# Latent attention: scores over high and low halves of q and k

## The chip, the cores and the metric

The kernel runs on one core of a Trainium2 chip. The metric is device time in microseconds (us) of one execution. A core has TensorE (PE in the profile, its weight loads PEld), VectorE (DVE), ScalarE (ACT), GpSimd (POOL) and SyncE (SP), which issues most DMAs. Each engine runs its own queue in order, and engines wait for each other by semaphores.

## The reference

The input is x, 8 sequences of 1024 tokens with 256 channels. A latent attention with 16 heads of width 16 is followed by a two-layer stack of windowed attention and gated MLP. The kernel normalises a token before each of the two parts and adds the part's result to its input. Cut to the part that the change touches:

```python
c_kv = x @ W_kv_down                                   # 256 -> 128
k_rope = rotary(c_kv @ W_k_rope)                       # 32 wide, shared by the heads
k = (c_kv @ W_k_up).reshape(B, T, 16, 16)
v = (c_kv @ W_v_up).reshape(B, T, 16, 16)
q = (x @ W_q).reshape(B, T, 16, 16)
q_rope = rotary(x @ W_q_rope)
scores = einsum('bqhd,bkhd->bhqk', q, k) + einsum('bqr,bkr->bqk', q_rope, k_rope)[:, None]
w = softmax(where(causal, -inf, scores / sqrt(48)))
out = einsum('bhqk,bkhd->bqhd', w, v).reshape(B, T, 256) @ W_o
```

## The kernel before

Two stages follow each other: `mla` (L155 on) does the latent attention of all 8 sequences, `local` the two layers after it. The end of `mla` and the start of `local` overlap. After both, a test over values collected on the way decides whether a general version is run as well; with these inputs it is not.

The exponential of a sum of scores is taken as a product: `rotary` (L402) computes the rotary scores, which all heads share, and ACT writes their exponentials into `er` once per block of 128 keys; a second exponential with the opposite sign (L409) serves the test alone, and both are summed along the way into `most` and `least`. POOL zeroes the masked triangle. For each head, `scores` (L421) makes the 16-wide products on PE, ACT takes the exponential into `pt` (L437), `turned` (L441) multiplies `pt` by `er` on DVE (L451), and `values` (L453) multiplies by v on PE (L462). v has a column of ones, so the sum of weights falls out beside the result; `finished` and `turn_back` divide by it and transpose on DVE, `out_add` multiplies by W_o and adds to x.

A unit of work is one or two of (c, g, kb): c is the half of the queries (512 columns), g a group of four heads, kb a block of 128 keys. Scores are transposed: keys on the partitions, queries along the columns. Four heads' products go at once to PE, each in its own 32 rows. As a head has 16 rows, keys are kept twice, in tiles `k` whose other 16 rows are zero (the mask of L372), so that one 32-row strip of q serves two heads. Blocks at the causal edge have 384, 256 or 128 query columns and are packed in pairs into one unit.

There are 36 units a batch (a batch is one sequence), 24 single and 12 paired, and one step of the loop takes one unit: the scores of unit s, then the multiplication of unit s-1, then the values of unit s-2, then what the table `beside` lists for this step. The table holds all other work of this sequence and of the next (who = 0 or 1; 2 loads and statistics of the one after it; -1 the output of the one before): normalisation, transposes, projections, rotary scores, output. PE, DVE, ACT and POOL keep the written order (`manual_schedule`); SP's order is left to the scheduler.

PSUM sets the ties between steps: a step's scores fill two tiles of two banks (`pscore`), which the exponentials of the step before must have left; everything listed in `beside` shares two single banks (`psum1`, by `bank`) in turn. `pt` has six buffers. All projections are cut by `times` (L198) into four matmuls of 32 columns of weights, which also run at once. During the second half of the last sequence, when no next one is prepared, the two single banks become a third score tile.

Of the kernel before, what the change touches and what calls it, by code (L numbers as in the profile page):

```python
# [29 lines left out]
F32 = mybir.dt.float32  # L30
AF = mybir.ActivationFunctionType
ALU = mybir.AluOpType
# [3 lines left out]
P = 128  # L36
# [45 lines left out]
def preln_mla_local_kernel(  # L82
# [72 lines left out]
    def mla(ctx: ExitStack, verdict):  # L155
# [85 lines left out]
        wq = wp.tile([P, 2, 2, 4, 2, HD], F32, name="wq")  # L241
        wk = wp.tile([P, 2, 4, 2, HD], F32, name="wk")
        mask = wp.tile([P, 2], F32, name="mask")
        for e in range(2):
            nc.vector.tensor_reduce(
                mask[:, e : e + 1], ident.rearrange("p (r e d) -> p r e d", e=2, d=HD)[:, :, e, :], AX.XY, ALU.add
            )
        for m in range(2):
            for e in range(2):
                cols = slice(128 * m + 64 * e, 128 * m + 64 * e + 64)  # L250
                nc.scalar.copy(
                    wq[:, :, m, :, e, :], wqnat[:, :, cols].rearrange("p c (r d) -> p c r d", d=HD)
                )
                nc.scalar.copy(wk[:, m, :, e, :], wknat[:, cols].rearrange("p (r d) -> p r d", d=HD))
        wq = wq.rearrange("p c m r e d -> p c m (r e d)")
        wk = wk.rearrange("p m r e d -> p m (r e d)")


# [10 lines left out]
        most = wp.tile([P, B * 12], F32, name="most")  # L269
        least = wp.tile([P, B * 12], F32, name="least")  # L270

        class Batch:


            def __init__(self, b):
                self.b = b
                self.sums = {}
# [4 lines left out]
            def statistics(self, n, part):  # L282
# [17 lines left out]
                self.found.append((mv, rstd))  # L300

            def normalise(self, n, part):
                mv, rstd = self.found[n]
                if part == 0:
                    if n == 0:
                        self.xn = []
                    self.xn.append(p1.tile([P, 4, D], F32, tag="xn", name=f"xn{self.b}_{n}", bufs=3))
                xn = self.xn[n]
                for i in (2 * part, 2 * part + 1):
                    nc.vector.tensor_scalar(  # L310
                        xn[:, i, :], self.x[:, 4 * n + i, :], mv[:, i, 0:1], rstd[:, i : i + 1],
                        ALU.subtract, ALU.mult,
                    )
# [40 lines left out]

            def query(self, m, n, c, part=None):
                if m == 0 and n == 1 and c == 0 and not part:
                    self.q = of[self.b % 2].tile([P, 2, T], F32, tag="q", name=f"q{self.b}")
                ps = self.dense(f"psq{m}_", [wq[:, 0, m, :], wq[:, 1, m, :]], self.xnc, n, c, part)
                if ps is not None:
                    on_a(self.q[:, m, HALF[n]], ps)  # L360

            def keys(self, m, n, part=None):

                if n == 0 and not part:
                    if m == 0:
                        self.k = []
                    for e in range(2):
                        g = 2 * m + e
                        self.k.append(of[self.b % 2].tile([P, T], F32, tag=f"k{g}", name=f"k{self.b}_{g}"))
                ps = self.dense(f"psk{m}_", [wk[:, m, :]], [self.ckvT], n, 0, part)  # L370
                for e in range(2) if ps is not None else ():
                    nc.scalar.activation(  # L372
                        self.k[2 * m + e][:, HALF[n]], ps, AF.Identity, scale=mask[:, e : e + 1]
                    )

# [26 lines left out]
            def rotary(self, c, kb):  # L402
# [3 lines left out]
                n = 12 * self.b + 8 * (1 - c) + kb  # L406
                nc.scalar.activation(er, ps[:, :w], AF.Exp, scale=SCALE, accum_out=most[:, n : n + 1])  # L407

                nc.scalar.activation(ps[:, :w], ps[:, :w], AF.Exp, scale=-SCALE, accum_out=least[:, n : n + 1])  # L409
                if q0 == kb * P:  # L410
# [3 lines left out]
                    )  # L414

# [5 lines left out]
            def scores(self, key, parts):  # L421
# [3 lines left out]
                for c, g, kb in parts:  # L425
                    q0, w, _ = self.block(c, kb)
                    for n in range(4):
                        rows = slice(32 * n, 32 * n + 32)
                        nc.tensor.matmul(  # L429
                            two[n // 2][:, n % 2, lo : lo + w], self.k[g][rows, kb * P : (kb + 1) * P],  # L430
                            self.q[rows, g // 2, q0 : q0 + w], start=True, stop=True,
                        )
                    lo += w
# [40 lines left out]
            def finished(self, c, g, oT):  # L474


                nat = late.tile([P, 16, 32], F32, tag="onat", name=f"onat{self.b}_{c}_{g}", bufs=3)
# [40 lines left out]
        for step, who, *what in (  # L518
            (0, -1, "out_add", 6, 1, 1), (0, 0, "query", 1, 1, 0),
            (1, 0, "query", 1, 1, 1),  # L520
            (2, 0, "value", 2),
            (3, 0, "keys", 1, 0), (3, 0, "keys", 1, 1, 0), (3, 1, "statistics", 1, 1),
            (4, 0, "keys", 1, 1, 1), (4, 0, "query", 0, 0, 0), (4, 1, "normalise", 0, 0),
            (5, 0, "query", 0, 0, 1), (5, 1, "normalise", 0, 1),
            (6, -1, "out_add", 0, 0), (6, 1, "normalise", 1, 0),
# [1314 lines left out]
```

## Time and profile before

| | us |
|---|---|
| median of 3 runs | 3347.74 (3345.59 to 3348.41) |
| span of the profiled execution | 3347.4 |
| scores of the first step, first record | 31.18 |
| one sequence in the steady part of `mla` (403.84 to 525.17) | 121.33 |
| PE, DVE, ACT, POOL busy in that stretch | 120.33, 107.69, 96.93, 9.49 |
| PE busy with L429, the scores, in that stretch | 45.34 |
| PE, DVE, ACT, POOL busy in the whole span | 3270.7, 2686.0, 1713.1, 1341.6 |

A sequence of `mla` thus takes 121 us and its 36 steps some 3.4 us each. The ends of matmuls are modelled in the profile and overlap the next start, so the time from one group's start to the next one's says more than a busy time. A matmul of fp32 operands shows as two records. A line of groups gives the line of code, the engine, the tiles written and read, the shapes and the count, then the busy time and the mean of one in ns, then the idle time ahead and what ended it. In shapes such as 32*128 the first number is the rows of the array in use, the second its columns.

### The profile page before, as it was taken

To read this page: it belongs to the slowest core of one execution; us is meant where nothing else is said; L and a number is where in the kernel's file an instruction comes from. 1 tells how busy PE (TensorE), PEld (TensorE's weight loads), DVE (VectorE), ACT (ScalarE), POOL (GpSimd) and SP (SyncE) were. 2 spreads that over 40 slices of the span, in tenths; PEclk is the share of its full clock that TensorE was granted. 3 is DMA by queue.
4 is the path that set the end of the run, shared out by engine and by line. 5 is a ranking of instruction groups with operands and counts; after the bars stand their busy time and mean duration, and the time that the engine had idled before them with its cause. 6 is when DMAs were issued, how large, how long until landed. Compare 5 with 4: busy or idle time off the path is not lost.

```text
span 3347.4 us, 79461 instructions
## 1 busy us (share of the span) xinstructions
PE 3270.7 (98%) x33826; PEld 1777.5 (53%) x33826; DVE 2686.0 (80%) x3993; ACT 1713.1 (51%) x2238; POOL 1341.6 (40%) x1031
## 2 busy tenths in 40 slices
PE   8999999999987899999999999999999999999998
PEld 2433333333333556666565666566666566665665
DVE  5888888888897887888878887777878778787773
ACT  6878878877862244434444434444444444344441
POOL 1000000000006655655655555555555555555540
PEclk9999999999998899999999999999999999999999
DMA  1000000000032444445344354444545444454431
GB/s 63 8 20 27 8 20 27 8 20 14 14 105 81 115 114 120 123 115 143 105 121 127 113 136 130 137 127 136 134 134 139 121 126 130 124 148 119 109 107 58
DMA packets 369290, 311.74 MB, mean 93 GB/s; under 512 B 154607, under 2 KB 333214, under 8 KB 368798
## 3 DMA queue, kind: packets, MB, share of 16 engines
q1 hardware_dynamic: 366942, 304.16, 33.1%
q8 instruction: 268, 4.39, 0.6%
q10 hardware_dynamic: 1984, 2.41, 0.2%
q14 instruction: 96, 0.79, 0.1%
HBM read 165.96 MB, written 140.51 MB: 92 GB/s over the span
## 4 chain that ended last, share of the span: by engine, by line
PE 90%; DVE 3%; ACT 2%; DMA 1%; issue 1%; SPq 1%; POOL 1%; ACTq 0%; DVEq 0%
PE ag L1088 17%; PE pair L859 13%; PE sc L429 9%; PE psy L1129 8%; PE acc L462 8%; PE psw L1005 7%; PE o L972 6%; PE pv L886 6%; PE pair L931 4%; PE psq L200 2%; PE psx L200 2%; PE s L980 2%; PE psR L200 2%; DVE pt L451 1%; PE psy L1135 1%
## 5 line engine op out<-in xcount | busy, mean ns | idle before, releaser
L451 DVE TENSOR_TENSOR pt<-pt,er 128x1024 f32<-128x1024 f32 x576 | 674.8, 1217 | 77.8 <-ACT pt L437 77.8
L437 ACT ACTIVATE pt<-sc 128x1024 f32<-128x1024 f32 x576 | 560.7, 1029 | 174.0 <-PE sc L429 161.6
L1088 PE MATMUL ag<-d,l 128*128 128x512 f32 x1408 | 640.4, 597 | 1.2 <-DVE xs L1009 0.8
L873 POOL TENSOR_TENSOR t<-t,t 128x1024 f32<-128x1024 f32 x128 | 302.0, 2360 | 792.0 <-DVE t L869 792.0
L937 ACT ACT_TABLE_LOAD x120 | 154.0, 1283 | 702.0 <-PE pair L931 702.0
L859 PE MATMUL pair<-l_qkv,xT 128*128 128x512 f32 x1024 | 469.2, 601 | 5.5 <-DMA xT<-zx 2.4
L1088 PEld LDWEIGHTS ag<-d,l 128*128 128x128 f32 x1408 | 262.2, 190 | 310.2 <-issue 278.1
L125 POOL TENSOR_TENSOR rn<-ss,half 128x16 f32<-128x16 f32 x128 | 373.4, 2917 | 13.7
L429 PE MATMUL sc<-q,k 32*128 32x512 f32 (+3 forms) x3072 | 369.9, 522 | 5.1 <-ACT pt L437 5.0
L462 PE MATMUL acc<-pt,v 128*32 128x512 f32 (+3 forms) x3072 | 332.9, 496 | 4.8 <-DVE pt L451 4.6
L859 PEld LDWEIGHTS pair<-l_qkv,xT 128*128 128x128 f32 x1024 | 193.7, 192 | 248.8 <-issue 207.6
L864 ACT ACTIVATE sq<-pair 128x1024 f32<-128x1024 f32 x128 | 131.0, 1023 | 333.2 <-issue 269.1
L866 DVE TENSOR_TENSOR t<-pair,l_cos 128x1024 f32<-128x1024 f32 x128 | 156.2, 1220 | 157.4 <-ACT sq L864 156.7
L1129 PE MATMUL psy<-l,hid 128*128 128x256 f32 x1280 | 281.5, 379 | 0.0
L1101 DVE SCALAR_TENSOR_TENSOR hid<-ag,l_b,ge 128x512 f32<-128x512 f32 x160 | 115.9, 724 | 196.3 <-ACT ge L1100 171.3
L1129 PEld LDWEIGHTS psy<-l,hid 128*128 128x128 f32 x1280 | 243.2, 190 | 46.7 <-issue 15.1
L937 ACT ACTIVATE pt<-pair 128x1024 f32<-128x1024 f32 (+1 forms) x256 | 234.9, 968 | 56.7 <-PE pair L931 55.4
L429 PEld LDWEIGHTS sc<-q,k 32*128 32x128 f32 x3072 | 157.3, 184 | 199.9 <-ACT pt L437 154.3
L411 POOL TENSOR_SCALAR_AFFINE_SELECT er<-er 128x128 f32<-128x128 f32 x64 | 51.5, 804 | 524.0 <-ACT er L407 524.0
L879 POOL TENSOR_TENSOR t<-t,rn 128x1024 f32<-128x1024 f32 x128 | 249.2, 1947 | 10.0
L972 PEld LDWEIGHTS o<-pt,v 128*32 128x32 f32 x7680 | 201.6, 110 | 88.0 <-issue 82.0
L886 PE MATMUL pv<-l_qkv,xT 128*128 128x512 f32 x512 | 240.6, 592 | 0.0
(132 smaller groups left out, 4876.8 us busy)
## 6 DMA issues: line engine op xcount, KB each, us to landing
z<-turned SPq DMA_DIRECT2D x512, 128.0 KB, 2.4
qkT<-z SPq DMA_DIRECT2D x128, 512.0 KB, 3.7
y<-xs SPq DMA_DIRECT2D x128, 128.0 KB, 2.6
h<-y SPq DMA_DIRECT2D x32, 512.0 KB, 4.0
zx<-turneds SPq DMA_DIRECT2D x120, 128.0 KB, 2.7
xT<-zx SPq DMA_DIRECT2D x240, 64.0 KB, 2.6
zh<-turnedh SPq DMA_DIRECT2D x120, 128.0 KB, 2.3
d<-zh SPq DMA_DIRECT2D x30, 512.0 KB, 3.2
```

The lines of the kernel that those rows point to most:

```text
L125: nc.gpsimd.tensor_tensor(out_, in_, half[:, :n], ALU.pow)
L429: nc.tensor.matmul(two[n // 2][:, n % 2, lo : lo + w], self.k[g][rows, kb * P : (kb + 1) * P], self.q[rows, g // 2, q0 : q0 + w], start=Tr ...
L437: nc.scalar.activation(pt, sc, AF.Exp, scale=SCALE)
L451: nc.vector.tensor_tensor(t, t, er.to_broadcast([P, 1024 // w, w]), ALU.mult)
L462: nc.tensor.matmul(self.acc[g][32 * n : 32 * n + 32, q0 - c * 512 :], self.v[:, kb, h * VW : h * VW + 32], pts[n // 2][:, n % 2, lo : lo + w],
L859: nc.tensor.matmul(qk[:, n].rearrange("p h d -> p (h d)"), self.left(i)[c], w["qkv"][:, c, n * INNER : (n + 1) * INNER], start=(c == 0), s ...
L873: nc.gpsimd.tensor_tensor(t1, t1, t2, ALU.add)
L886: nc.tensor.matmul(pv, self.left(i)[c], self.w["qkv"][:, c, 2 * INNER :], start=(c == 0), stop=(c == 1))
L937: nc.scalar.activation(pt[:, :, : n * P], flat[:, :, : n * P], AF.Exp, scale=-1.0)
L972: nc.tensor.matmul(o[32 * j : 32 * j + 32, g, a, :], vs[m][:, h * DH + a * 32 : h * DH + a * 32 + 32], pts[m][g][:, place(j), off : off + ...
L1088: nc.tensor.matmul(ps.rearrange("p (s a t) -> p s a t", a=4, t=32), w["1"][:, c, i, :], d[:, c], start=(c == 0), stop=(c == 1),)
L1129: nc.tensor.matmul(ps[:, t, :], hid[:, i, cols], w["2"][:, i, :], start=(t == i == 0), stop=False)
```

## The change

- q and k are split in two. The projection's result is copied to a float32r tile (`halves`), which holds the high half; one step later (`low`) TensorE adds minus that half to the same PSUM bank, a matmul with the negative unit matrix `minus`, and what is left is copied as the low half.
- Both halves are then moved by DMA from SP's queue (`place_q`, `place_k`) into tiles of another layout: a head's 32 rows hold high and low parts of k row by row in turn, and for q the same part twice. `scores` makes two float32r products per head, over the low part of q and then the high one, in place of one fp32 product. The masked copies of k and the rearranged weights `wq` and `wk` are gone.
- The normalisation moves from DVE to ACT, with a shift that POOL computes.
- The second exponential of `rotary` and both accumulated sums are gone; in their place squares of the rotary parts (`squares`, ACT) are summed by PE and reduced by DVE (`reach`) once a sequence.
- `xn` and `onat` have two buffers in place of three, and the table lists the projections anew, with `low` entries that are done right after the step's scores.

```diff
+        minus = wp.tile([P, P], F32R, name="minus")
+        nc.scalar.mul(minus, ident, -1.0)
...
+                shift = small.tile([P, 4], F32, tag="shift", name=f"shift{b}_{n}")
+                nc.gpsimd.tensor_tensor(shift, mv[:, :, 0], rstd, ALU.mult)
+                nc.gpsimd.tensor_scalar(shift, shift, -1.0, None, ALU.mult)
+                self.found.append((shift, rstd))
...
                 for i in (2 * part, 2 * part + 1):
-                    nc.vector.tensor_scalar(
-                        xn[:, i, :], self.x[:, 4 * n + i, :], mv[:, i, 0:1], rstd[:, i : i + 1],
-                        ALU.subtract, ALU.mult,
+                    nc.scalar.activation(
+                        xn[:, i, :], self.x[:, 4 * n + i, :], AF.Identity, scale=rstd[:, i : i + 1],
+                        bias=shift[:, i : i + 1],
                     )
...
+            def halves(self, ps, then, *args):
+                t = p1.tile([P, 2, 512], F32R, tag="halves", name=f"halves{self.b}_{then.__name__}{args}", bufs=2)
+                on_a(t[:, 0], ps)
+                self.pending = ps, t, then, args
+
+            def low(self):
+                ps, t, then, args = self.pending
+                nc.tensor.matmul(ps, minus, t[:, 0], start=False, stop=True, skip_group_check=True)
+                on_a(t[:, 1], ps)
+                then(t.bitcast(F32), *args)
...
+            def place_q(self, t, m, n):
+                for g in (2 * m, 2 * m + 1):
+                    q = of[g % 2].tile([P, 2, 512], F32, tag=f"q{g}{n}", name=f"q{self.b}_{g}_{n}")
+                    for s in range(2):
+                        nc.sync.dma_start(q[s : P : 2], t[64 * (g % 2) : 64 * (g % 2) + 64])
+                    self.q[g, n] = q.bitcast(F32R)
...
-                for e in range(2) if ps is not None else ():
-                    nc.scalar.activation(
-                        self.k[2 * m + e][:, HALF[n]], ps, AF.Identity, scale=mask[:, e : e + 1]
-                    )
+                self.halves(ps, self.place_k, m, n)
+
+            def place_k(self, t, m, n):
+                for g in (2 * m, 2 * m + 1):
+                    k = of[self.b % 2 if (m, n) == (0, 0) else 0].tile(
+                        [P, 512], F32, tag=f"k{g}{n}", name=f"k{self.b}_{g}_{n}"
+                    )
+                    for s in range(2):
+                        nc.sync.dma_start(k[s : P : 2], t[64 * (g % 2) : 64 * (g % 2) + 64, s])
+                    self.k[g, n] = k.bitcast(F32R)
...
-                nc.scalar.activation(er, ps[:, :w], AF.Exp, scale=SCALE, accum_out=most[:, n : n + 1])
-
-                nc.scalar.activation(ps[:, :w], ps[:, :w], AF.Exp, scale=-SCALE, accum_out=least[:, n : n + 1])
+                nc.scalar.activation(er, ps[:, :w], AF.Exp, scale=SCALE)
...
+            def squares(self, n):
+                t = (self.rq, self.rk)[n]
+                sq = p1.tile([P, T], F32, tag="xn", name=f"sq{self.b}_{n}", bufs=2)
+                nc.scalar.activation(sq, t, AF.Square)
+                self.sq = getattr(self, "sq", []) + [sq]
+
+            def reach(self):
+                ps = bank(f"reach{self.b}")
+                for i, four in enumerate(QUARTER):
+                    nc.tensor.matmul(ps[four], ones, self.sq[i // 2][:, HALF[i % 2]], start=True, stop=True)
+                nc.vector.tensor_reduce(norms[:, self.b : self.b + 1], ps, AX.X, ALU.max)
...
-                    for n in range(4):
-                        rows = slice(32 * n, 32 * n + 32)
-                        nc.tensor.matmul(
-                            two[n // 2][:, n % 2, lo : lo + w], self.k[g][rows, kb * P : (kb + 1) * P],
-                            self.q[rows, g // 2, q0 : q0 + w], start=True, stop=True,
-                        )
+                    k = self.k[g, kb // 4][:, kb % 4 * P : (kb % 4 + 1) * P]
+                    q = self.q[g, c][:, :, q0 - c * 512 :]
+                    for h in (1, 0):
+                        for n in range(4):
+                            rows = slice(32 * n, 32 * n + 32)
+                            nc.tensor.matmul(
+                                two[n // 2][:, n % 2, lo : lo + w], k[rows], q[rows, h],
+                                start=(h == 1), stop=(h == 0),
+                            )
...
-            (3, 0, "keys", 1, 0), (3, 0, "keys", 1, 1, 0), (3, 1, "statistics", 1, 1),
-            (4, 0, "keys", 1, 1, 1), (4, 0, "query", 0, 0, 0), (4, 1, "normalise", 0, 0),
-            (5, 0, "query", 0, 0, 1), (5, 1, "normalise", 0, 1),
-            (6, -1, "out_add", 0, 0), (6, 1, "normalise", 1, 0),
...
+            (2, 0, "low"), (2, 0, "value", 2),
+            (3, 0, "keys", 1, 0), (3, 1, "statistics", 1, 1),
+            (4, 0, "low"), (4, 0, "keys", 1, 1), (4, 1, "normalise", 0, 0),
+            (5, 0, "low"), (5, 0, "query", 0, 0, 0), (5, 1, "normalise", 0, 1),
+            (6, 0, "query", 0, 0, 1), (6, 1, "normalise", 1, 0),
+            (7, 0, "low"), (7, -1, "out_add", 0, 0), (7, -1, "out_add", 0, 1),
...
+            (10, 0, "query", 1, 0, 0), (10, 1, "normalise", 1, 1),
+            (11, 0, "query", 1, 0, 1), (11, 1, "turn", 0, 0),
+            (12, 0, "low"), (12, 0, "rotary", 0, 0), (12, 1, "turn", 0, 1),
...
+            (22, 1, "query", 0, 1, 0, 1), (22, 1, "query", 0, 1, 1), (22, 1, "squares", 0),
+            (23, 1, "low"), (23, 1, "keys", 0, 0), (23, 2, "statistics", 0, 0), (23, 1, "squares", 1),
+            (24, 1, "low"), (24, 1, "value", 0),
...
+            (27, 1, "low"), (27, 1, "rotary", 1, 0),
...
-            (32, 0, "out_add", 4, 1),
+            (32, 0, "out_add", 4, 1), (32, 1, "reach"),
```

## The prediction

> **What bounds the kernel now.** I read the page's totals first, then the stages, the groups, the timeline of one step and the waits.
>
> ```profile
> PE 3270.7 (98%) x33826; PEld 1777.5 (53%) x33826; DVE 2686.0 (80%) x3993; ACT 1713.1 (51%) x2238; POOL 1341.6 (40%) x1031
> PE 90%; DVE 3%; ACT 2%; DMA 1%; issue 1%; SPq 1%; POOL 1%; ACTq 0%; DVEq 0%
> ```
>
> The chain that ended last is TensorE's, and the lines concerned (L429, L462, L200) work only in the first 1000 us. The busy times of stretches there (columns: stretch, length, then busy time of each engine; 121.33 us from 403.84 is one whole batch, the next two lines split a batch into steps 4 to 25 and steps 26 to 3, the last is the tail of the last batch):
>
> ```profile
> 100.00:900.00 800.00, 793.99 (x8576) 312.34 (x8572) 707.64 (x891) 640.11 (x993) 59.86 (x65) 1.00 0.05 17
> 403.84:525.17 121.33, 120.33 (x1298) 47.25 (x1297) 107.69 (x138) 96.93 (x150) 9.49 (x10) 1.00 0.06 19
> 416.99:491.56 74.57, 73.57 (x781) 27.69 (x777) 64.93 (x80) 56.07 (x79) 4.76 (x5) 1.00 0.07 23
> 491.56:538.32 46.76, 46.76 (x524) 19.56 (x520) 42.76 (x59) 40.86 (x73) 4.73 (x5) 1.00 0.04 13
> 940.00:1000.00 60.00, 51.16 (x406) 17.36 (x404) 54.35 (x79) 37.13 (x43) 3.94 (x6) 0.94 0.48 146
> ```
>
> PE is full in every stretch, but DVE stands at 89% and ACT at 80% right behind, DVE at 91% in steps 26 to 3. In the tail DVE is at 91% and PE is not full: nothing taken from PE helps there. A plain step in the timeline (start, length, engine, line):
>
> ```profile
> 479.06 1.14 PE L429 MATMUL sc<-q,k 32*128 32x512 f32 x8
> 480.13 1.07 PE L462 MATMUL acc<-pt,v 128*32 128x512 f32 x8
> 480.23 1.94 ACT L437 ACTIVATE pt<-sc 128x1024 f32<-128x1024 f32 x2 [1.41 <-PE sc L429]
> 481.01 1.47 PE L200 MATMUL psq<-xnT,wq 128*32 128x256 f32 x16
> 482.42 0.74 PEld L429 LDWEIGHTS sc<-q,k 32*128 32x128 f32 x16 [0.84 <-ACT pt L437]
> ```
>
> Taken from start to start, four heads' scores (4 fp32 products, 8 records) take 1.07 us, their values 0.88, projections 1.41; the exps take 1.94 and start 1.17 after the scores. Per step DVE multiplies twice (L451, 1217 ns each, 2.31 for a pair back to back). One batch by groups (busy, mean ns):
>
> ```profile
> L451 DVE TENSOR_TENSOR pt<-pt,er 128x1024 f32<-128x1024 f32 x73 | 85.5, 1216 | 7.6 <-ACT pt L437 7.6
> L437 ACT ACTIVATE pt<-sc 128x1024 f32<-128x1024 f32 x72 | 70.0, 1029 | 20.6 <-PE sc L429 20.4
> L429 PE MATMUL sc<-q,k 32*128 32x512 f32 x192 | 29.6, 640 | 0.0
> ```
>
> **What the Trainium skill says.** "TensorE: Matmul & The Clock Gate", section "Back-to-back issue gap": a warm matmul of N columns takes N/2.4 + 2.5 ns, 216 for 512. The trace's fp32 product is two records (192 for the batch's 24 groups of four heads at 512 columns), and a quad of value records (four column groups at once) takes 0.88/2 = 0.44 us, about twice that: fp32 costs some 427 per record. Same page, "LDWEIGHTS (loading the stationary operand)": columns/1.2 ns, 107 for 128. The score quad takes 0.535 = 0.427 + 0.108, so it agrees, and these loads aren't hidden. The rate of float32r is shown by no run here: it is the large unknown. "ScalarE: Activation LUTs", section "What ACT_TABLE_LOAD costs": 186 + 0.833 per column ns, 93 more for each per-partition operand, 93 of overlap. The trace agrees: copies of 512 at 593, the masked key copy (one such operand) at 693.
>
> **The change, part by part (per batch; 36 steps).**
>
> 1. *Scores.* 48 groups of four heads: 24 of 512 columns, 8 each of 384, 256 and 128. Each goes from two fp32 quads to two float32r quads; the weight loads stay. If float32r streams a column per cycle, a 512 quad falls from 0.535 to 0.216 + 0.107 = 0.32 and the saving per quad is N/2.4: 24×2×0.213 + 8×2×(0.160+0.107+0.053) = 10.2 + 5.1 = 15.4 us. Ends: 0 (as fast as an fp32 record), and a loss of 41 (as slow as a whole fp32 product: each quad doubles; sum now about 24×1.07 + 8×(0.85+0.64+0.43) = 41). I take the column per cycle: a full fp32 product is made here of two double-priced records[...]. Narrow groups (128) could be slower; 1 us or so.
> 2. *The low halves.* 8 matmuls 128x128x512 float32r: 0.216 + 0.107 + 0.1 assumed for the change of tile shape (0 to 0.2) = 0.42, so +3.4. Each waits for ACT's copy of the step before and stands ahead of values on PE; that copy comes before the step's exps in ACT's queue, so I cost the wait at 0, about 0.6 (one copy) if it is late.
> 3. *reach*: 4 fp32 matmuls, one 512 quad pair, +0.9 on PE, +0.7 on DVE (as L346, 0.69). Splitting projections anew moves PE work between steps, sum unchanged.
> 4. *DVE*: normalise leaves (8×406 ns, 2.9 busy in this batch): 107.7 − 2.9 + 0.7 = 105.5.
> 5. *ACT*: the second exp of rotary and all accumulator reads leave (64 groups' sum: 29.9+8.1+6.8+4.8+21.2 and 22.0 over 8 batches, −11.6); the masked key copies and q copies leave (40.7+19.0 over 8, −7.5); 16 half copies come at 593 (+9.5), eight normalisations at 186+213+186−93 = 0.49 (+3.9), two squares of 1024 at 1.03 (+2.1). Sum 96.9 − 3.6 = 93.3.
> 6. *POOL*: two small operations per four tiles, a step or more ahead of use; 0. *DMA*: 32 moves a batch on SP's queue, 16 of 256 KB and 16 of 128 KB, 6 MB in 115 us where the DMA share is 0.06. Moves of 256 KB land in 2.4 us here (x2d<-x); four at once I put at 6. First use comes 8 steps or more (25 us) after the low half. SP's stores and loads of x now stand among them: each waits on work already due. The halves buffers (two) are rewritten about two steps after their DMAs started (6 us): tight only for the second keys, at most 1 us. So 0 to 1.
>
> PE's sum: 121.3 − 15.4 + 3.4 + 0.9 = 110.2; DVE 105.5; ACT 93.3. PE still leads, but three queues in order, tied within a step, don't reach the largest sum. Taking the two halves of a batch:
>
> - Steps 26 to 3 (14 steps): these hold three of a batch's four pairs of closing transposes, three of four statistics and two of four output additions. PE falls to 46.8 − 14×0.43 + 2×0.42 + 0.9 = 42.5, DVE is 42.8 + 0.7 = 43.5 and becomes the bound; the values of a step come two steps after its scores, which lets PE lead DVE by some 2 us. 41.5 to 44: gain 2.8 to 5.3.
> - Steps 4 to 25 (22 steps): PE is 74.6 − 16×0.43 − 6×0.43 + 6×0.42 = 67.7. Two costs come on top. At step 12 the rotary scores take the bank that this step's low copy frees, and with two banks in turn PE waits for ACT behind both exps: about 3.2 us after the step's start instead of 1.9, 1.2. And ACT is overfull in steps 4 to 6 (exps 1.94, two half copies 1.14, two normalisations 0.98: 4.06, 3.5, 3.5, against PE's 2.9, 2.9, 2.5) and 22 to 24 (two squares, 10.7 against 8.7): 4.8 in all, of which perhaps 1 is absorbed each time, so 0 to 3. Total 69 to 72: gain 2.6 to 5.6.
>
> Per batch 5.4 to 10.9, taken 8.2. Seven batches and the first 16 steps of the last one count, 7.4: 61 us. The start: the rotary part before the first step is held up by ACT (idle of 0.4 to 0.8 on PE after psR), whose work halves there; against that stand two squares, the half copies and the DMA before the first scores. I take 0, ±4. The tail and the local layers stay. The profiled span is 3347.4, the median 3347.7: 3347.7 − 61 = 3287.
>
> **The rivals.**
>
> A. *float32r streams no faster than an fp32 record* (or slower): step 1 gives nothing, PE is 121.3 + 8×0.63 + 0.9 + 1.2 = 128.5, 7.2×7.4 = +53: 3400; at the whole product's price another 41×7.4, near 3700. It ends slower from the point where a 512 quad costs over some 0.48 (the additions are 5.5, spread over 96 quads of 370 columns on average). For: nothing here prices it. Against: the argument of one pass. 0.14. (That the new test of norms fails and sends the run into the general path, is under 0.01 in it: the inputs' largest sum of squares over the rotary rows is about 147, the limit 271.)
>
> B. *The engines' ties eat the gain*: ACT's full steps and DVE's closing steps add up unabsorbed, the halves' buffers wait for DMAs. The waits show that PE and ACT already wait for each other in most steps:
>
> ```profile
> ACT pt L437 <- PE sc L429: 135.5, 158, 2.2
> PEld sc L429 <- ACT pt L437: 120.6, 200, 0.8
> ```
>
> 2 to 5 a batch: 3312 to 3335, about 3325. 0.13.
>
> C. *The ties loosen*: shorter scores let the exps start 0.5 earlier (a loop of 1.94 + 0.55 in place of 1.17), so ACT's fullness is absorbed and PE leads DVE freely. The bound is then the larger sum, about 108: 13×7.4 = 98, 3250. 0.13.
>
> **How the numbers follow.** Forecast 0.60, its own range 3262 to 3312. Range 3245 to 3342: the forecast, all of B (0.13) and half of C (0.065) make 0.80; left out are A and C's lower half. A change of under 0.2% (7 us) can't be told from none in this kernel. Faster: 0.60 + 0.13 of C + 0.12 of B; same 0.01, B's rest; slower A's 0.14.
>
> **What would show it.** Scores L429's successor: start to start 0.65 for a 512 group; if about 1.07, A. Low matmuls about 0.4 each. A batch period of 110 to 116. DVE over 95% busy in steps 26 to 3; PE's idle before rotary at step 12, and before scores in steps 5 to 7 and 23 to 25, released by ACT. No wait of scores on q's or k's DMA past the first step; if there is one, the DMA term was wrong. The local layers equal within 1 us.

## The result and the profile after

The changed kernel takes 3294.14 us (median of 4 runs, 3292.07 to 3297.83), the kernel before 3346.91 beside it: a ratio of 0.984, 95% interval 0.983 to 0.986. The profiled execution has a span of 3290.3 against 3347.4, so 57.1 us are to be found between the two traces.

The totals of the page and the shares of the chain that ended last, after:

```profile
PE 3196.2 (97%) x33762; PEld 1763.2 (54%) x33762; DVE 2668.6 (81%) x3934; ACT 1712.4 (52%) x2055; POOL 1342.9 (41%) x1064
PE 84%; DVE 6%; ACT 4%; DMA 2%; issue 2%; SPq 1%; POOL 0%; ACTq 0%; DVEq 0%
```

TensorE gives up 6 points of the chain to DVE, ACT, DMA and issue. By stretches (columns as in the prediction: stretch, length, busy time of PE, PEld, DVE, ACT, POOL, clock, DMA share, GB/s; the six middle sequences, one whole sequence, its steps 4 to 25, and steps 26 to 3):

```profile
100.00:837.00 737.00, 720.21 (x8365) 294.99 (x8363) 681.19 (x833) 624.74 (x825) 60.23 (x87) 1.00 0.29 72
502.51:616.51 114.00, 111.33 (x1292) 45.63 (x1291) 105.68 (x131) 96.64 (x128) 9.64 (x14) 1.00 0.30 75
514.77:585.10 70.33, 68.81 (x772) 27.51 (x768) 63.01 (x73) 60.21 (x81) 4.50 (x7) 1.00 0.38 94
471.10:514.77 43.67, 42.50 (x527) 18.03 (x524) 42.67 (x59) 36.42 (x49) 5.13 (x7) 1.00 0.17 45
```

A sequence takes 114.0 (121.33 before), steps 4 to 25 take 70.3 (74.6), steps 26 to 3 take 43.7 (46.8). In the last line DVE is busy for 42.67 of 43.67 us: there it has become the bound. The DMA share is 0.30 in place of 0.06. A plain step in the timeline (start, length, engine, line):

```profile
560.44 0.74 PE L455 MATMUL sc<-q,k 32*128 32x512 f32 x8
561.10 1.07 PE L488 MATMUL acc<-pt,v 128*32 128x512 f32 x8
561.21 1.94 ACT L463 ACTIVATE pt<-sc 128x1024 f32<-128x1024 f32 x2 [0.48 <-PE sc L455]
561.99 1.47 PE L201 MATMUL psrq<-xnT,wqr 128*32 128x256 f32 x16
563.39 0.30 PEld L455 LDWEIGHTS sc<-q,k 32*128 32x128 f32 x8 [0.84 <-ACT pt L463]
```

Four heads' scores take 0.66 from start to start (1.07 before), and their exponentials follow the scores' start by 0.77 (1.17 before). Everything else in the step is as it was. The waits of the middle sequences (engine, line, waited for: us in total, times, longest):

```profile
PEld sc L455 <- ACT pt L463: 101.4, 155, 0.8
ACT pt L463 <- PE sc L455: 86.3, 106, 2.4
PEld acc L488 <- DVE pt L477: 38.3, 84, 1.1
PE acc L488 <- DVE pt L477: 3.6, 6, 0.6
```

The values' weight loads wait for DVE's multiplications, but that is not new: over 800 us of the kernel before these waits are 72.6 us (0.8 at the longest). New is the last line: once a sequence TensorE itself stands still before the values until DVE has multiplied. The kernel before has no such line.

Cut at the first scores of sequences 1 and 7 and at the first transposes of the local layers, the two traces differ like this (us):

| part | forecast | measured |
|---|---|---|
| start and sequence 0 (161.17, then 159.17) | -8.2 | -2.0 |
| six middle sequences (728.0, then 685.0) | -49.2 | -43.0 |
| last sequence, to the first local transposes (133.1, then 123.2) | -3.3 | -9.9 |
| from there to the end (2325.1, then 2323.0) | 0 | -2.1 |

So the sum comes out near the forecast, but the first two parts gained less than forecast and the third more. The experiments look for the cause of each.

### The profile page after: what moved, and what is told of

Same layout as the page of the kernel before. It is cut to its first block, busy times and chain, and to the rows that moved or that the text cites. A ratio compares the mean times of both kernels' runs of the same rounds, so it can differ in the third digit from the quotient of the medians.

```text
span 3290.3 us, 79693 instructions
## 1 busy us (share of the span) xinstructions
PE 3196.2 (97%) x33762; PEld 1763.2 (54%) x33762; DVE 2668.6 (81%) x3934; ACT 1712.4 (52%) x2055; POOL 1342.9 (41%) x1064
## 4 chain that ended last, share of the span: by engine, by line
PE 84%; DVE 6%; ACT 4%; DMA 2%; issue 2%; SPq 1%; POOL 0%; ACTq 0%; DVEq 0%
PE ag L1115 17%; PE pair L886 13%; PE psy L1156 8%; PE psw L1032 7%; PE o L999 6%; PE acc L488 6%; PE pv L913 6%; PE sc L455 5%; PE pair L958 4%; DVE pt L477 3%; PE s L1007 2%; PE psx L201 2%; PE psq L201 1%; PE psR L201 1%; ACT pt L463 1%
## 5 line engine op out<-in xcount | busy, mean ns | idle before, releaser
L488 PE MATMUL acc<-pt,v 128*32 128x512 f32 (+3 forms) x3072 | 345.6, 496 | 11.2 <-DVE pt L477 10.0
L964 ACT ACTIVATE pt<-pair 128x1024 f32<-128x1024 f32 (+1 forms) x256 | 235.0, 968 | 57.1 <-PE pair L958 55.8
L455 PE MATMUL sc<-q,k 32*128 32x512 f32 (+3 forms) x3072 | 245.1, 380 | 4.4 <-ACT pt L463 3.3
L1032 PE MATMUL psw<-l_o,oT 128*128 128x256 f32 x1024 | 240.2, 388 | 0.0
L999 PE MATMUL o<-pt,v 128*32 128x128 f32 x7680 | 237.0, 274 | 2.6 <-POOL pt L966 2.4
```

The source lines that it names most:

```text
L455: nc.tensor.matmul(two[n // 2][:, n % 2, lo : lo + w], k[rows], q[rows, h], start=(h == 1), stop=(h == 0),)
L488: nc.tensor.matmul(self.acc[g][32 * n : 32 * n + 32, q0 - c * 512 :], self.v[:, kb, h * VW : h * VW + 32], pts[n // 2][:, n % 2, lo : lo + w],
L964: nc.scalar.activation(pt[:, :, : n * P], flat[:, :, : n * P], AF.Exp, scale=-1.0)
L999: nc.tensor.matmul(o[32 * j : 32 * j + 32, g, a, :], vs[m][:, h * DH + a * 32 : h * DH + a * 32 + 32], pts[m][g][:, place(j), off : off + ...
L1032: nc.tensor.matmul(ps[:, i, :], oT[:, c, i * P : (i + 1) * P], self.w["o"][:, c, :], start=(c == 0), stop=(c == 3),)
```

## Experiments

### What the rate of float32r is worth, and where PE still sets the pace

Two kernels keep the whole change, but make one product for each head in place of two, and so leave out the product with the low half of q. In the first it is an fp32 product, in the second float32r.

```diff
-                    for h in (1, 0):
-                        for n in range(4):
...
+                    for n in range(4):
+                        rows = slice(32 * n, 32 * n + 32)
+                        nc.tensor.matmul(
+                            two[n // 2][:, n % 2, lo : lo + w], k[rows].bitcast(F32), q[rows, 0].bitcast(F32),
+                            start=True, stop=True,
+                        )
```

(The second has the same lines without the two bitcasts.)

> The changed kernel with one fp32 product per head (high part of q only; the product with q's low part is left out), so each group of four heads has two fp32 quads as before the change, and all else is as changed. Theory (float32r's rate is the gain): a 512 group goes from 0.67 back to 1.07 us start to start, PE's sum grows by about 15 us a batch and leads everywhere: a batch of 125 to 128 in place of 114, total 3375 to 3400. Rival (the gain comes from ACT's and DVE's relief): within 20 us of the changed kernel's 3294.

> The changed kernel with the float32r product over q's high part alone (the product with the low part is left out): a 512 group falls to 0.33, PE loses some 13 us a batch. Theory (DVE is the bound in steps 26 to 3, ACT's full steps and buffer waits share steps 4 to 25): steps 26 to 3 stay at 43 to 44, steps 4 to 25 fall from 71.7 by 2 to 4: total 3262 to 3280. Rival (PE alone still bounds): a batch falls by 12 or more, total near 3200.

One fp32 product: 3364.1, one float32r product: 3266.5 (one run each). The sequences take 123.1 and 110.5, against 114.0 with two float32r products. The first is some 10 us under the range of its theory (a sequence of 125 to 128, 3375 to 3400), and far from its rival. The groups of the scores in one sequence, kernel with one fp32 product (busy us, mean ns):

```profile
L454 PE MATMUL sc<-q,k 32*128 32x512 f32 x193 | 29.6, 640 | 0.0
L454 PE MATMUL sc<-q,k 32*128 32x128 f32 x64 | 4.2, 269 | 0.0
```

The same two groups in the changed kernel:

```profile
L455 PE MATMUL sc<-q,k 32*128 32x512 f32 x194 | 19.8, 445 | 0.0
L455 PE MATMUL sc<-q,k 32*128 32x128 f32 x64 | 3.5, 243 | 0.0
```

Two float32r products are faster than one fp32 product by 9.2 us a sequence, some 70 us over eight: without the rate, the change would be slower than the kernel before, by 1.8 a sequence. That is rival A's mechanism, put in place by hand, and it gives 3364 rather than the 3400 forecast for it. So the rate is what makes the change faster.

The second kernel shows where PE still sets the pace. It takes another 3.5 off a sequence, all of it from steps 4 to 25 (66.9 against 70.3); steps 26 to 3 stay at 43.6: there less work for PE brings nothing. One whole sequence of it:

```profile
376.50:486.90 110.40, 105.23 (x1100) 40.38 (x1098) 105.44 (x131) 95.61 (x128) 9.69 (x14) 1.00 0.31 78
```

PE is busy for 6.1 us less than in the changed kernel, and DVE for as long; the sequence becomes 3.6 shorter. The total is inside the theory's range, but the price of one product was mis-sized in it: a group of 512 columns takes 0.44, not 0.33, and the product that is left out was 6.1 us of a sequence, not 13.

### The normalisation: ACT's full steps, or the start

```diff
-                    nc.scalar.activation(
-                        xn[:, i, :], self.x[:, 4 * n + i, :], AF.Identity, scale=rstd[:, i : i + 1],
-                        bias=shift[:, i : i + 1],
+                    nc.vector.tensor_scalar(
+                        xn[:, i, :], self.x[:, 4 * n + i, :], mv[:, i, 0:1], rstd[:, i : i + 1],
+                        ALU.subtract, ALU.mult,
                     )
```

> The changed kernel with the normalisation back on DVE (shift on POOL gone). Theory (ACT is overfull in steps 4 to 6): ACT loses 4.4 us a batch, 1.1 in each of steps 4, 5, 6 and 10, DVE gains 3.2 where it has slack; steps 4 to 25 fall by 1.5 to 2.5, steps 26 to 3 stay: total 3276 to 3286. Rival (DVE's sum is the bound): plus 3 us a batch, 3310 to 3316.

3287.5, ratio to the kernel before 0.982 (0.981 to 0.984). A sequence takes 113.9 as before the edit, though ACT has 3.3 us less to do and DVE 2.4 more. The theory that ACT is overfull in steps 4 to 6 is not supported, and the total is just above its range. The gain is at the start: sequence 1 begins at 152.57 in place of 159.17. ACT's timeline there, changed kernel:

```profile
10.76 4.04 ACT L299 ACTIVATE xn<-x,shift,rstd 128x256 f32<-128x256 f32 x8 [1.70 <-POOL shift L288]
14.83 1.07 ACT L79 COPY xnT<-psn 128x512 f32<-128x512 f32 x2
```

With the normalisation on DVE:

```profile
11.08 1.23 ACT L79 COPY xnT<-psn 128x512 f32<-128x512 f32 x2 [2.11 <-PE psn L204]
```

At the start ACT has nothing else to do. The shift on POOL and eight normalisations in a row on ACT stand between the statistics and the first transposes, and the copies of those transposes come 3.75 us later. The first scores start at 45.08 in place of 40.34, and sequence 0 is itself 1.9 shorter with DVE.

### The halves' buffers

In one of the six middle sequences step 5 takes 6.41 us, in the others 4.72. ACT and PE in that step, changed kernel:

```profile
404.54 0.59 ACT L79 CAST alves_place_k(1, 1)_4826<-psk 128x512 fp32r<-128x512 f32 x1 [1.95 <-DMA q<-alves_place_q(1, 1)_4698]
405.17 0.19 PEld L355 LDWEIGHTS psk<-alves_place_k(1, 1)_4826,minus 128*128 128x128 f32 x1 [2.07 <-ACT alves_place_k(1, 1)_4826 L79]
```

ACT cannot write the second keys' halves before the DMA that empties the buffer has landed, PE waits for ACT, and the step's exponentials wait behind the copy in ACT's queue. The low copy of q(1,1) began at 396.19, SP took 3.07 us to issue its four moves, and the last landed at about 404.5. In the other five sequences ACT waits in the same place, for 1.1 to 1.3 us.

```diff
-                t = p1.tile([P, 2, 512], F32R, tag="halves", name=f"halves{self.b}_{then.__name__}{args}", bufs=2)
-                on_a(t[:, 0], ps)
+                t = p1.tile([P, 512], F32R, tag="high", name=f"high{self.b}_{then.__name__}{args}", bufs=3)
+                on_a(t, ps)
...
+                r = p1.tile([P, 512], F32R, tag="low", name=f"low{self.b}_{then.__name__}{args}", bufs=2)
+                on_a(r, ps)
```

(Each half of q also moves by a DMA of its own, and to make room two weights of the start share another tile's space and the closing sums have one buffer.)

> The changed kernel with the high and the low halves in tiles of their own, three of the high and two of the low (room for them comes from two start-up weights and the closing sums, which share tiles), so that the second keys' high copy at the end of step 4 no longer waits for the DMAs of q(1,1). Each q half moves by a DMA of its own, 128 KB each. Theory (this wait delays step 5's exps and costs what step 5 shows over a plain step, about 4.7 against 3.3): 1.0 to 2.0 us less per batch, 3280 to 3287. Rival (another wait, or PE's own sum in steps 4 to 8, takes its place): 3292 to 3296, step 5 shorter and a later step longer by as much.

3292.0 (ratio 0.983, 0.981 to 0.985), hardly less than the changed kernel. ACT's wait is gone, yet the usual sequence is only some 0.1 shorter and its step 5 still takes 4.7; the start loses 1.0. The rival holds: something else was there all along.

The slow step is gone too (the six sequences take 682.7 in place of 685.0, 1.6 of it in this one), but that is not the buffers' doing. Two other kernels leave the buffers as they are, have the same late copy in the same sequence (a wait of 1.97), and no slow step: 4.76 with the normalisation on DVE, 4.73 with the squares moved (next section). What they do not share is the clock. The slow step (columns as above), and the same step with the squares moved:

```profile
402.81:409.22 6.41, 4.78 (x27) 1.45 (x25) 6.38 (x8) 4.68 (x8) 1.61 (x3) 0.73 0.47 121
400.04:404.77 4.73, 3.08 (x28) 1.09 (x26) 4.70 (x6) 2.98 (x5) 1.62 (x3) 1.00 0.65 162
```

The values and the projection behind them, first in the slow step, then with the squares moved:

```profile
405.60 1.98 PE L488 MATMUL acc<-pt,v 128*32 128x512 f32 x8
407.20 2.10 PE L201 MATMUL psq<-xnT,wqnat 128*32 128x512 f32 x8
402.85 1.13 PE L488 MATMUL acc<-pt,v 128*32 128x512 f32 x8
403.74 1.10 PE L201 MATMUL psq<-xnT,wqnat 128*32 128x512 f32 x8
```

From start to start they take 1.60 and 2.02 in place of 0.89 and 1.03, together 1.7 more, which is what the step is longer. Why the granted clock fell there is not shown.

The chain through a usual step 5 in the new kernel (start, length, what; step 4 starts at 513.77, step 5 at 517.21, step 6 at 521.92):

```profile
513.04 2.27 DVE pt L479 x2
515.31 0.66 DVE bnst L277 x2
...
516.39 0.61 DVE oT L520
...
517.76 2.28 DVE pt L479 x2
520.08 0.62 PE acc L490 x2
```

It runs on DVE. The work that makes DVE the bound of steps 26 to 3 is not finished at step 4; the multiplications are late, and PE waits for them with its values until step 5 is over.

### The squares

```diff
-            (21, 1, "rope_k", 1), (21, 1, "query", 0, 1, 0, 0),
-            (22, 1, "query", 0, 1, 0, 1), (22, 1, "query", 0, 1, 1), (22, 1, "squares", 0),
-            (23, 1, "low"), (23, 1, "keys", 0, 0), (23, 2, "statistics", 0, 0), (23, 1, "squares", 1),
+            (21, 1, "rope_k", 1), (21, 1, "squares", 0), (21, 1, "query", 0, 1, 0, 0),
+            (22, 1, "query", 0, 1, 0, 1), (22, 1, "query", 0, 1, 1),
+            (23, 1, "low"), (23, 1, "keys", 0, 0), (23, 2, "statistics", 0, 0),
...
-            (28, 1, "rotary", 1, 1),
+            (28, 1, "rotary", 1, 1), (28, 1, "squares", 1),
```

> The changed kernel with its two squares at steps 21 and 28 instead of 22 and 23. Theory (ACT is overfull in steps 22 to 24, where two squares, two keys and query copies and eight exps stand together): steps 22 to 24 together 0.7 to 1.3 us shorter, nothing back elsewhere, 3284 to 3289. Rival (PE or DVE makes up for it within the next steps, as with the normalisation): 3292 to 3296.

3289.6 (ratio 0.982, 0.980 to 0.983). Steps 4 to 25 take 69.1 in place of 70.3, steps 26 to 3 take 44.0 in place of 43.7: 0.9 a sequence. The theory holds in the main: step 24 falls from 3.75 to 3.10 and step 25 from 3.08 to 2.59, so ACT was too full there; but 0.3 comes back in steps 26 to 3, where one square now stands, and the total is just above the theory's range.

### The end of the last sequence

It became 9.9 shorter, where 3.3 were forecast. Up to the scores of step 17 the gain is 3.0, nearly all that was forecast. From there to those of step 23 it is 10.4, and 3.6 of that are lost again up to the first local transposes. These six steps in the kernel before:

```profile
941.71:970.06 28.35, 21.12 (x100) 4.40 (x97) 22.91 (x44) 12.66 (x13) 3.53 (x5) 0.88 0.75 220
```

and in the changed kernel:

```profile
893.66:911.57 17.91, 15.67 (x100) 3.77 (x96) 16.19 (x15) 12.02 (x14) 0.00 (x0) 1.00 0.73 241
```

DVE has 6.7 us less to do in them, and its idle time falls from 5.4 to 1.7. Of the 29 instructions that are gone most are the statistics and the normalisation of the first x tile of the local layers. In the kernel before these stand between the last multiplications (its first statistics at 944.89), in the changed kernel directly behind the last one (at 952.91). The idle time is the wait for the local layers' first loads. Kernel before, ACT and DVE:

```profile
952.02 1.02 ACT L437 ACTIVATE pt<-sc 128x1024 f32<-128x1024 f32 x1 [4.46 <-DMA l_qkv<-in_L_ffn_wqkv_dram]
954.01 1.22 DVE L686 TENSOR_TENSOR l_cos<-l_cos,l_fcos 128x1024 f32<-128x1024 f32 x1 [4.47 <-DMA l_fcos<-in_L_ffn_k_scale_dram]
```

Changed kernel, the same two instructions:

```profile
902.04 1.94 ACT L463 ACTIVATE pt<-sc 128x1024 f32<-128x1024 f32 x2 [2.64 <-DMA l_o<-in_L_ffn_wo_dram]
902.50 1.23 DVE L713 TENSOR_TENSOR l_cos<-l_cos,l_fcos 128x1024 f32<-128x1024 f32 x1 [1.72 <-DMA l_sin<-in_xpos_sin_dram]
```

The loads were issued 54.3 us after the last sequence's start before, and 48 after it in the changed kernel. The chain that ended last has these pieces in the six steps of the kernel before, among others:

```profile
945.65 9.67 DMA l_sin<-in_xpos_sin_dram
955.72 3.08 DMA l_fsin<-in_L_ffn_k_scale_dram
963.43 1.92 POOL rstds L125
965.37 1.38 DVE xs L761 x4
```

and in those of the changed kernel:

```profile
894.96 7.53 DMA l_sin<-in_xpos_sin_dram
902.50 1.23 DVE l_cos L713
903.73 7.04 DVE pt L477 x7
```

So the loads on this chain fell from 12.8 to 7.5, and the local statistics stand on it behind the last multiplication instead (from 952.99 on), which is part of what is lost again. This names the path; it does not say what each piece is worth. The granted clock is 0.88 before and 1.00 after, but no work of PE lies on the chain there in the kernel before, so the clock is not shown to have cost anything. Four kernels take this apart, all from the kernel before. One has the new test alone (the squares and `reach`, with the second exponential and the sums gone):

```diff
-                nc.scalar.activation(er, ps[:, :w], AF.Exp, scale=SCALE, accum_out=most[:, n : n + 1])
-
-                nc.scalar.activation(ps[:, :w], ps[:, :w], AF.Exp, scale=-SCALE, accum_out=least[:, n : n + 1])
+                nc.scalar.activation(er, ps[:, :w], AF.Exp, scale=SCALE)
...
+            (32, 0, "out_add", 4, 1), (32, 1, "reach"),
```

> The kernel before with the new test alone: no second exponential and no accumulated sums in the rotary steps, squares and reach in their place; scores, layout and normalisation as before. Theory: the batch stays bound by PE at 121.3 to 122.2 (reach adds 0.9); the start and the tail of the stage gain, since the rotary part of the first batch is held by ACT and the local layers' first loads wait for the old test's end: 2 to 6 and 6 to 10 us; total 3333 to 3345. Rival (ACT's relief is a main part of the gain): 3320 or less.

3350.7 (ratio 1.001, 1.000 to 1.002). The start gains 1.4 us, the loads are issued at 49.8, and the end is where it was: first local transposes 133.3 us after the last sequence's start (133.1). Earlier loads alone brought nothing, and the new test, on its own, loses 0.2 a sequence.

One issues the first local tables on SP's queue:

```diff
-            queue = nc.sync if l else nc.scalar
+            queue = nc.sync
```

> The kernel before with the first local layer's tables and inputs issued on SP's queue instead of ACT's. The changed kernel's last batch is 11.9 us shorter up to the last multiplication, the prediction had 3.3. Theory (these loads are issued late from ACT's queue, in the trace at 943.5 us, and ACT and DVE stop for them inside the last batch): the tail shrinks by 5 to 8 us, 3338 to 3342. Rival (the stops are idle time that was there anyway, the multiplications' own number decides): 3345 to 3348.

3345.6, ratio 0.9992 (0.9985 to 0.9999). The first local transposes come at 127.9, 5.2 earlier: ACT no longer stops, and of these six steps (24.3 in place of 28.4) DVE is idle for 1.4. So the stops were on the path, though the time fell by about 3 us only, which is inside the range of the rival.

Two move the local statistics behind the last multiplication. The only edit of the first is the place at which a pool is opened, which changes SBUF addresses; the second opens two pools ahead of all others, on top of the new test. The edit of the first:

```diff
-        px = ctx.enter_context(tc.tile_pool(name="l_x", bufs=3))
         pxT = ctx.enter_context(tc.tile_pool(name="l_xT", bufs=2))
         p1 = ctx.enter_context(tc.tile_pool(name="l1", bufs=1))
         p2 = ctx.enter_context(tc.tile_pool(name="l2", bufs=2))
+        px = ctx.enter_context(tc.tile_pool(name="l_x", bufs=3))
```

> The kernel before with the local layers' pool of x tiles opened after their other pools, so that it gets other SBUF addresses; nothing else is edited. By the written order of DVE's instructions, the first local tile's statistics and normalisation (8.2 us on DVE between the multiplications of steps 17 to 23 in the trace of before) then stand behind the last multiplication, as they do in the changed kernel. Theory (this order, set by where the memory of that tile comes free, is what shortens the last batch beyond the batch's own gain): the last multiplication 8 to 12 us earlier, the first local transposes 4 to 8 us earlier, about 3340 to 3344. Rival (that work only filled idle time of DVE, the late loads set the pace): last multiplication at most 3 us earlier, transposes not earlier, 3345 to 3349.

> The kernel before with the new test (as in the run with the test alone), and the local layers' pools opened in another order, so that by the written order the first local tile's statistics and normalisation stand behind the last multiplication, while its x is loaded as early as before (in the run of the kernel before with x tiles last, x was loaded only at 128.7 us of the last batch, and the local layers began later). The loads of the local tables are issued some 5 us earlier than before, since the old test's tiles no longer gate them. Theory (both together shorten the last batch: loads that start early, and DVE free of the local statistics in steps 17 to 23): last multiplication 6 to 10 us earlier than in the kernel before, first local transposes 4 to 8 us earlier, 3339 to 3344. Rival (the order only shifts work behind the last multiplication): transposes within 2 us, 3345 to 3350.

3353.5 and 3353.3, ratio 1.002 for both (1.001 to 1.003): slower. Steps 17 to 23 shrink to 25.2 and 24.8. Counted from the last sequence's start, the last multiplication ends 3.6 and 4.6 earlier, but the first local transposes come 3.7 and 2.1 later. In these two kernels the statistics start 15 to 16 us behind the last multiplication, after the closing of the last heads; in the changed kernel they start 0.5 us behind it and run while the closing waits for PE. Taken away from between the multiplications, they also leave the waits for the loads bare: in the first of them DVE is idle for 7.7 of the 25.2.

So neither the earlier loads nor the moved work gives the gain alone, nor these two together in the order of the last run, and the theory put forward for that run falls. What the traces show of the changed kernel is three things at once: tables issued 6 us earlier, x loaded only 101.4 us after the sequence's start (49.8 before), and the statistics right behind the last multiplication. (The multiplications done ahead of the wait for the first table are nearly as many: 36 of the sequence's 72, and 35 before.) That all three are needed is argued, not shown.

### All edits together

Normalisation on DVE, high and low tiles apart, squares moved, local loads on SP's queue, and the rotary block of step 12 kept away from the low copy whose bank it takes:

```diff
-            (9, 0, "value", 3),
-            (10, 0, "query", 1, 0, 0), (10, 1, "normalise", 1, 1),
-            (11, 0, "query", 1, 0, 1), (11, 1, "turn", 0, 0),
-            (12, 0, "low"), (12, 0, "rotary", 0, 0), (12, 1, "turn", 0, 1),
-            (13, 0, "rotary", 0, 2), (13, 1, "down", 0, 0),
+            (9, 0, "rotary", 0, 2), (9, 0, "query", 1, 0, 0),
+            (10, 0, "query", 1, 0, 1), (10, 1, "normalise", 1, 1),
+            (11, 0, "low"), (11, 0, "value", 3),
+            (12, 0, "rotary", 0, 0), (12, 1, "turn", 0, 0),
+            (13, 1, "turn", 0, 1), (13, 1, "down", 0, 0),
```

> All of it together: normalisation on DVE, separate high and low tiles, squares at 21 and 28, the rotary scores of step 12 a step away from the low copy whose bank they take, local loads on SP's queue. If the waits named are what the batch has over its largest engine sum: start 6.6 less, 3 to 4 us less per batch, 3255 to 3270. If DVE, which has 108 us of a batch with the normalisation on it, takes their place as the bound: 3280 to 3288, with a period of 113 to 114.

3277.9 (3276.3 to 3278.2), ratio to the kernel before 0.978 (0.977 to 0.980), the fastest of the kernels that do the whole work, and between the two ranges given. One whole sequence of it:

```profile
490.02:602.92 112.90, 111.18 (x1290) 44.98 (x1288) 108.18 (x139) 93.53 (x120) 11.75 (x10) 1.00 0.30 76
```

The start gains 7.9 us, of which the normalisation alone had 6.6. A sequence gains 1.1, not 3 to 4. PE is busy for 111.2 and DVE for 108.2 of its 112.9 us; which of the two holds the rest is not shown. Two versions of it with the local pools in other orders, so that the scaling of the local tables goes behind the last multiplication as well:

> The version with all edits together, and the local layers' working pool opened first, so that by the written order the scaling of the first local tables (two multiplications of 1.2 us on DVE, which wait for loads) stands behind the last multiplication of the scores too. If the waits on these loads (about 2 us on DVE and 2.6 us on ACT in steps 18 to 20 of the last batch) were on the path: 3 to 5 us less than the version without it, 3273 to 3276. If the first local transposes only come later behind the last multiplication by as much: 3277 to 3281.

> The version with all edits together, and the local layers' pools of x opened first, so that their x is loaded before their weights, and the scaling of the tables stands behind the last multiplication. If the order of loads and of the first local work sets the few us between the last batch and the local layers: 3272 to 3276. If what leaves the last batch comes back in front of the first local transposes, as with the working pool first: 3278 to 3287.

3286.0 and 3279.7: no gain, and the first is 8 us slower. The last multiplication ends 2.3 and 1.6 us earlier after the last sequence's start, but the first local transposes come 1.1 and 1.9 later; in the trace of the first, the part behind them is 5.5 longer as well.

## Why the prediction was right, and where it was wrong

The total is right for the reason given, the rate of float32r, but that it came so near is in part luck. Against the forecast the start and the middle sequences came out 12.4 us too long, and the tail and the local layers 8.7 too short.

**Scores (step 1): right in kind, mis-sized.** In a step of 512 columns the two float32r products of four heads take 0.67 us from start to start. The price worked out from the Trainium skill ("TensorE: Matmul & The Clock Gate", sections "Back-to-back issue gap" and "LDWEIGHTS (loading the stationary operand)"), an estimate, was 0.32 for each, so the trace agrees. A product alone takes 0.44, though, so the second adds 0.23, little more than the 0.216 that the page's formula gives for 512 columns: the load was not paid with every product, as the prediction had it. In the kernel before, too, the groups of 256 columns in a paired step start 0.216 apart after the first, with no time for a load between them. With each record counted from its start to the next one's, the score records take 42.8 us of a sequence before and 30.2 after. That is 12.7 saved where the forecast had 15.4. The 24 steps of 512 columns saved 8.7 of 10.2, the four of 256 columns 2.0 of 1.7, and the eight that pair 384 with 128 columns 2.0 of 3.4. This mis-sized term is larger than the gain that a sequence lacks; the paragraph on the halves of a sequence says what made up for it.

**Low halves and `reach` (steps 2 and 3): right.** The eight low matmuls take 0.425 to 0.432 each, 3.4 in all; `reach` takes 0.97.

**DVE, ACT (steps 4 and 5).** DVE's sum is 105.7 (105.5 forecast), ACT's 96.6 (93.3). The normalisations take 0.49 from start to start, as priced. The lengths of all ACT records together fell by 2.3 where 3.6 were forecast, and as records overlap, by 13.6 us before and by 11.6 after, the busy time fell by 0.3 only. ACT's sum did not set the pace: 3.3 less of it left the sequence as it was.

**The halves of a sequence.** Steps 26 to 3 at 43.7 (41.5 to 44) and steps 4 to 25 at 70.3 (69 to 72) are where they were forecast. In the first DVE is the bound, as said. In the second one named cause holds, one falls and one was not tried alone. ACT was too full at the squares, 1.2 in these steps. The normalisations in steps 4 to 6 cost nothing, since taking them off ACT left the sequence as it was. Step 12 takes 3.88, in the version with all edits 3.23, but there steps 9 and 13 become longer by 0.3 to 0.4. What the split hid is that the stretch bound by DVE runs on through step 5. In the sum: 121.33, less 12.7 for the scores, 3.4 and 1.0 for the additions, and 1.4 that the value records take longer, as they wait for DVE. This gives 114.4; 114.0 were measured. A sequence gained 7.3 (7.2 in the mean, with the one slow step) where 8.2 were taken. Here two misses cancel as well: PE's sum is 113.0 where 110.2 were forecast, but the sequence is only 1.0 longer than that sum, where 2.9 were allowed for waits.

**DMA (step 6): right.** No scores waited for q or k past the first step. The second keys are the tight place, as named, "at most 1 us": ACT waits there for 1.1 to 1.3, once for 1.95, but with that wait gone a sequence is only some 0.1 shorter. The 1.6 of the one slow step go with its clock.

**The start: wrong.** It was taken as 0, ±4. With the steady pace taken off (159.17 less 114.0, against 161.17 less 121.33) it costs 5.3. The step that failed is that the normalisation's price on ACT was counted for the steady part alone, where other work hides it. At the start nothing does, and taking it off ACT again gave 6.6.

**The tail: wrong in the other direction.** "The tail and the local layers stay" left out that the addresses of tiles change, and with them the time at which the local layers' tiles come free, the issue of their loads and the place of their first work in DVE's queue. It gave 6.6 more than forecast, all of it behind step 17. Of this the waits for loads are shown to be on the path: without ACT's stops the kernel before reached the transposes 5.2 earlier. The rest is open, as said above.

**The local layers** came out 2.1 shorter, outside the 1 us named. The code is the same, and in the kernels run here this part takes 2323 to 2331, so nothing can be read from it.

The rivals: A's rate was not the chip's. B's range leaves a gain of 2 to 5 us a sequence; 7.3 were measured, and what is missing is the mis-sized scores, not ties. C did not happen: with PE's sum at 113.0 its 108 could not be reached, and DVE bounds steps 26 to 3.

## What to carry to other kernels

A price that is hidden in the steady part must be paid where the cover is missing: cost each moved instruction once for the loop and once for the start. When the bound moves to another engine, its stretch does not end where its extra work ends but where its backlog is worked off. And a change that frees or moves SBUF tiles can move loads and whole groups of instructions at a stage's border; compare the written order of the queues there before calling a part unchanged. Before a wait is blamed for one slow step, look at the granted clock of that step, and for the same wait in a step that is not slow.

## What was unexpected in the hardware

- At 128 columns float32r brought little. The last four matmuls of a step that pairs 384 with 128 columns took 0.200 us in fp32 and in float32r alike, from the last of them to the start of the next group.
- SP took 3.07 us to issue four moves from SBUF to SBUF of 64 partitions each. They had landed some 7.0 us after the copy that they wait for, and 7.7 in the sequence with the slow step; the prediction had put four at 6.
- In one step the granted clock was 0.73 on average, and the values and a projection took 1.60 and 2.02 us in place of 0.89 and 1.03.
